# Last pass of a two-layer convolution kernel: its transfers on one queue, its norm chain in seven stages, and a tile's reads dealt over a convolution step

## Chip, cores, metric

The kernel runs on one core of a Trainium2 chip. The metric is device time in microseconds (us). The engines are TensorE (PE for its matmuls, PEld for its weight loads), VectorE (DVE), ScalarE (ACT), GpSimd (POOL) and SyncE (SP). Each executes its own instructions in order. Transfers (DMA) are issued by an engine's instruction stream, here mostly by SyncE and POOL, and so stand in order with everything else on that engine; they all run on the core's 16 DMA engines.

## What is computed

The input x is 8 x 96 x 96 x 192 in float32. There are two residual layers. The part that matters here is the second:

```python
x = x + L0(_gn(x))                       # layer 0
y = conv7x7_depthwise(_gn(x)) + dw_bias  # layer 1; _gn is a group norm over 32 groups of 6 channels
mu = mean(y, axis=-1); var = mean((y - mu)**2, axis=-1)
y = (y - mu) * rsqrt(var + 1e-6) * ln_gamma + ln_beta
y = gelu(y @ w0 + b0)                    # 192 -> 768
y = y @ w1 + b1                          # 768 -> 192
out = x + y * gamma
```

Layer 0 projects 192 channels to 384, applies a 3x3 depthwise convolution and four exponential scans, normalises over the channels and projects back to 192 channels.

## The kernel before

**Stages.** The first three stages compute layer 0. They end with the residual stage (`load_c`, `block_c`, `finish_c`), which writes the sum to the DRAM tensor X (`X1_d`, one part for each half of the batch) and gathers the group norm's sums. Then comes the depthwise convolution of layer 1 (letter d in the code), then the last stage (letter e): norm over the channels, the expansion with gelu ("first layer"), the contraction ("second layer"), the residual and the output.

**Convolution.** It works on 32 tiles `todo[n]`, 16 blocks of 12 channels (`i`) for each half of the batch (`hf`). For a tile, `load_raw(n, t)` reads three pieces `raw` (t = 0, 1, 2), each in two halves of 384 KB, one issued by SyncE and one by POOL; `load_band(n)` reads the weight matrix `band` (624 KB) by SyncE where the block's index i is even and by POOL where it is odd, into one half of the partitions; `scale_steps(n)` gives 24 scalings `xin<-raw` (eight for each piece; they apply the group norm; DVE L838, or ACT L836 for tile 1 and for tiles from 19 on) and ends with a DVE copy of the band into the other half of the partitions (L842). `conv_d(n, c)` is called for c = 0..5: 24 matmuls (L1167) into two PSUM banks, which ACT empties into `yo` with the bias (L1177). `store_d(n)` writes `yo` to the DRAM tensor Y: three stores by SyncE and three by POOL, of which one each has 810 KB and the others 27 KB.

**Buffers of raw.** Before the change, pieces of tile 0 and pieces 0 and 1 of odd tiles and of tiles from 19 on have two buffers in the pool `early`, which lives from before the residual stage on. Even tiles (2 to 18) and piece 2 of odd tiles have four buffers in the pool `own`, which lies where the residual stage's tiles were and opens when that stage is over.

**Order of the convolution.** All order is written out by hand (`tc.manual_schedule()`). Tiles 0 to 18 (`N1` = 19) run alone, with no work of the last stage beside them ("convolution alone"). In the loop over n, each turn issues `store_d(n - 1)`, `load_band(n + 1)`, `load_raw(n + 2, t)` for the three pieces, `scale_steps(n + 1)`, and then the six steps of `conv_d(n, c)`. As soon as tile 15 is stored, the first half of the batch is complete in Y, and the last stage can begin. So in turn n = 16 `load_y(0)` is issued, all 41 steps at once, behind `store_d(15)` and `load_band(17)` and ahead of `load_raw(18, t)`; in turn 18 the norm chain of e-tile 0 is put ahead of the convolution's steps; after the loop come `load_y(1)`, `store_d(18)`, `load_band(19)` and two pieces of raw 19. The bank of PSUM is taken in a ring of eight.

**Last stage.** It has 72 e-tiles u, two for each of the 36 pieces of Y. `load_y(n)` gives 41 steps: one that makes the tiles `ya` and `yb` (two buffers each) and 40 reads from Y by SyncE (32 of 60 KB, L1226, and 8 of 16 KB, L1232, one after each four). The first 20 reads fill `ya`, the others `yb`. `load_r(n)` reads the residual `r` (1536 KB, SyncE, L1243), and `bias_r(n)` adds the output bias to it on POOL (L1249). `norm_steps_e(u)` gives the chain of the norm, before the change in six stages: `sums` (DVE, L1305), `mean` (DVE), `center` (two subtracts on DVE, L1298, and two squares on ACT, L1318), `squares` (DVE, L1324), `powers` (DVE, and a power on POOL, L1330, that gives `rs`), `scale` (small DVE copies `m<-rs` that wait for POOL, and two multiplies at L1298). `turn_in(u, k)`, k = 0, 1, 2, transposes 32x32 blocks on DVE into `yT` (L1351). `first_layer(u, part, ..)` has the expansion's matmuls (L1366 and L1376) and the gelu on ACT (L1385), in three parts in the first half of the e-tiles and in two in the second half. `second_layer(u, k, ..)`, k = 0..3, has 48 matmuls (L1396), the residual add on DVE (L1407, `xo`) and the output's store by POOL (L1415).

**Mixed stage.** A step of the loop over u has the first layer of u, the second layer of u - 1 in four quarters, the norm chain of u + 2 (its last stage, `scale`, in the next step) and the turns of u + 1. Between them `slot()` is called five times. From u = 2 on a slot takes one entry of the list `slots` until that is empty. Each convolution tile from 19 to 31 has nine entries: three with eight scalings each, which also issue the next raw reads (the entry of piece 0 issues `raw (n, 2)`, those of pieces 1 and 2 issue pieces 0 and 1 of tile n + 1), and six with one `conv_d(n, c)` each on two PSUM banks of its own (`ps_y`), of which the last also issues `store_d(n)` and `load_band(n + 1)`. So tile n + 1 begins one slot after tile n's store. A slot also takes up to seven steps of a pending `load_y`. Those are put in line in even steps u, ahead of the fourth slot, so they fall into the fourth and fifth slot of an even step and the first four of the odd step. `load_r` comes after the first slot of odd steps and `bias_r` after the third. Before the change a slot issues its steps of `load_y` first and its convolution entry second. When `slots` is empty, nothing but the last stage is left.

Of the kernel before, what the change touches and what calls it, by code (L numbers as in the profile page):

```python
# [101 lines left out]
def conv_blocks_kernel(  # L102
# [31 lines left out]
    nc = tc.nc  # L134
# [655 lines left out]
    def load_raw(n, t):  # L790

        hf, i = todo[n]
        own = 0 < n < N1 and (n % 2 == 0 or t == NT - 1)
        raw = d_pools[own].tile(
            [128, NH, NV, GC, WQ], F32, tag="raw", name="raw", bufs=4 if own else 2
        )
        raws[n, t] = raw
        row = NGC * NV * GC * WQ
        run = NV * GC * WQ
        x1 = X1_d[hf]  # L800
        for g, eng in enumerate((nc.sync, nc.gpsimd)):
            src = bass.AP(
                tensor=x1.tensor,
                offset=x1.offset + (2 * t + g) * HG * PH * row + i * run,
                ap=[[row, 64], [ROWS * row, NH], [1, run]],
            )
            eng.dma_start(
                raw[g * 64 : (g + 1) * 64].rearrange("q b a c v -> q b (a c v)"), src
            )

    def load_band(n):
# [5 lines left out]
        (nc.sync, nc.gpsimd)[g].dma_start(  # L817
# [4 lines left out]
    def scale_steps(n):  # L822
# [4 lines left out]
        def scale(t, k, b):  # L827
# [7 lines left out]
            if n == 1 or n >= N1:  # L835
# [89 lines left out]
    with ExitStack() as ph:  # L925
# [143 lines left out]
        with tc.manual_schedule():  # L1069
            weights = load_weights()  # L1070
            for u in range(n_u + 1):
# [7 lines left out]
                if u == n_u - 20:  # L1079
                    load_band(0)  # L1080
                    for t in range(NT - 1):
                        load_raw(0, t)
                    first_d += scale_steps(0)
                    for k, (n, t) in enumerate(((0, 2), (1, 0), (1, 1))):
                        first_d.insert(
                            (k + 1) * 8 + k, lambda n=n, t=t: load_raw(n, t)
                        )
# [97 lines left out]
    def store_d(n):  # L1185
# [5 lines left out]
        for k, eng in enumerate((nc.sync, nc.gpsimd)):  # L1191
# [64 lines left out]
    def norm_steps_e(u):  # L1256
# [57 lines left out]
        def center():  # L1314
            apply(ALU.subtract)
            t_["sq"] = sq = sp.tile([128, NH, WE + HV, CK], F32, tag="sq", name="sq", bufs=1)
# [24 lines left out]
        return [sums, mean, center, squares, powers, scale]  # L1341
# [78 lines left out]
    with tc.manual_schedule():  # L1420
        with tc.tile_pool(name="d_own", bufs=1, side="right", **by_tile) as own:
            d_pools[1] = own
            load_raw(1, NT - 1)
            load_band(1)
            norms = norm_c(1, bank)
            for n in range(N1):
# [4 lines left out]
                if n == NI:  # L1431
                    for step in load_y(0):
                        step()
# [4 lines left out]
                if n == N1 - 1:  # L1438
                    for step in norm_steps_e(0):
                        step()  # L1440
                else:
# [3 lines left out]
                    for step in scale_steps(n + 1):  # L1445
                        step()
                for c in range(GS):
                    conv_d(n, c)
            for step in load_y(1):
                step()  # L1450
# [26 lines left out]
        def slot():  # L1477

            for step in loads[:7]:
                step()  # L1480
            del loads[:7]
            if slots and u >= 2:
                for step in slots.pop(0):
                    step()
# [4 lines left out]
        last = norm_steps_e(1)  # L1489
        while len(last) > 1:  # L1490
            last.pop(0)()
        bias_r(0)
        for u in range(n_u + 1):
# [6 lines left out]
            scale_next, last = last[-1], norm_steps_e(u + 2) if u + 2 < n_u else [lambda: None] * 6  # L1500
            first_layer(u, 0, parts, pool)
            scale_next()
            last.pop(0)()
# [4 lines left out]
            turn_in(u + 1, 0)  # L1508
            last.pop(0)()
            slot()  # L1510
            if early_half:
                first_layer(u, 1, parts, pool)
            turn_in(u + 1, 2)
            second_layer(u - 1, 1, pool)
            last.pop(0)()
            slot()
# [5 lines left out]
            if t == 1 and n + 1 < n_y:  # L1522
                bias_r(n + 1)
            if not early_half:
                first_layer(u, 1, parts, pool)
            second_layer(u - 1, 2, pool)
            last.pop(0)()
# [3 lines left out]
            last.pop(0)()  # L1531
            second_layer(u - 1, 3, pool)
            slot()
# [47 lines left out]
```

## Time and profile before

| | us |
|---|---|
| median of three runs | 5646.87 |
| lowest and highest of them | 5640.79, 5653.08 |
| the profiled execution | 5650.55 |
| its span (first to last instruction) | 5648.7 |
| PE busy | 5332.8 |
| DVE busy | 3620.2 |
| ACT busy | 2583.7 |
| POOL busy | 2372.4 |
| end of the residual stage's matmuls | 2643 |
| first and last matmul of the convolution (L1167) | 2643.8, 4133 |
| first matmul of the first layer (L1366) | 3033.9 |
| first matmul of the second layer (L1396) | 3079.4 |

The page divides the span into 40 equal slices of 141 us and gives for each the busy share of an engine in tenths; PEclk is the clock granted to TensorE, in tenths of full speed. In a listing by time, a line has its start in us from the span's start, its length, the engine, the line of the code, the operation with what it writes and reads, and how many like instructions are merged in it. Where an engine was idle before it, square brackets give for how long and what released it. `SPq` is SyncE issuing a transfer: its length is the issue, not the transfer. A group's row gives busy time, the mean length in ns, and the idle time of the engine before its instructions with what ended it.

### The profile page before, as it was taken

The page shows a single profiled execution, that of the slowest core. Times are in us where ns is not written, and L with a number is a line of the kernel's source. Part 1 is how long each engine was busy: PE and PEld are TensorE (multiplying, and loading weights), DVE is VectorE, ACT ScalarE, POOL GpSimd, SP SyncE. Part 2 cuts the span into 40 slices and gives each one's busy share as a digit, 9 for nine tenths or more (in the row PEclk, how much of TensorE's full clock was granted, in tenths as well). Part 3 has the DMA queues.
Part 4 walks back from the last instruction along what each step waited for, and adds up shares of the span by engine and source line. Part 5 has one row for each costly group of instructions (what it writes and reads, how often), then busy time and mean ns, then how long its engine had stood idle before and what let it go on. Part 6 is the DMA issues. An engine that isn't in the chain of part 4 may idle for free. (4 is left out here: it accounts for less than half of the span.)

```text
span 5648.7 us, 108168 instructions
## 1 busy us (share of the span) xinstructions
PE 5332.8 (94%) x42206; PEld 3354.0 (59%) x42206; DVE 3620.2 (64%) x6738; ACT 2583.7 (46%) x5762; POOL 2372.4 (42%) x2122
## 2 busy tenths in 40 slices
PE   6999989999998999998776998989999999999999
PEld 3666633333333999997343555555566677666667
DVE  5556449999998455555455554555567677767764
ACT  2444447777776566565332444434433333333332
POOL 1111128888887555554222332322333333333332
PEclk9999979999999999999887999999999999999999
DMA  7999869999997899999995445455433332233331
GB/s 208 281 287 270 239 176 244 246 244 244 244 246 207 261 295 288 281 289 264 270 269 132 118 118 113 119 121 135 111 82 85 87 86 77 78 85 91 82 78 40
DMA packets 793200, 1015.29 MB, mean 180 GB/s; under 512 B 331840, under 2 KB 674417, under 8 KB 790641
## 3 DMA queue, kind: packets, MB, share of 16 engines
q1 hardware_dynamic: 696664, 640.98, 43.9%
q0 software_dynamic: 90064, 365.17, 20.6%
q8 instruction: 333, 5.46, 0.4%
q10 hardware_dynamic: 5960, 2.22, 0.2%
q14 instruction: 179, 1.46, 0.1%
HBM read 603.70 MB, written 419.95 MB: 181 GB/s over the span
## 5 line engine op out<-in xcount | busy, mean ns | idle before, releaser
L1396 PEld LDWEIGHTS hp<-w1g,g 128*128 128x128 f32 x6912 | 1117.9, 190 | 140.7 <-issue 71.8
L1396 PE MATMUL hp<-w1g,g 128*128 128x192 f32 x6912 | 1174.9, 329 | 0.0
L1385 ACT ACTIVATE g<-hp,b0g 128x512 f32<-128x512 f32 x864 | 518.2, 690 | 771.0 <-PE hp L1376 771.0
L1366 PE MATMUL hp<-yT,w0w 128*128 128x512 f32 x1728 | 788.4, 602 | 22.9 <-DVE yT L1351 13.4
L1415 POOL DMA_DIRECT2D out_dram<-xo x288 | 211.6, 735 | 1393.2 <-DVE xo L1407 1360.2
L1007 PE MATMUL po<-wc,mt 128*128 128x193 f32 x3456 | 683.6, 333 | 2.1 <-DVE x1c L1024 1.8
L1407 DVE TENSOR_TENSOR xo<-hp,r 128x384 f32<-128x384 f32 x288 | 227.8, 791 | 689.7 <-PE hp L1396 688.3
L600 PE MATMUL pl<-pin,band 34*32 34x380 f32 (+1 forms) x13824 | 636.4, 494 | 18.8 <-DMA pin<-P_d 18.8
L1167 PE MATMUL hp<-xin,band 63*64 63x372 f32 (+1 forms) x4608 | 453.9, 529 | 176.5 <-DMA band<-Z_d 63.2
L674 POOL TENSOR_TENSOR mo<-mo,z 128x768 f32<-128x768 f32 x286 | 598.0, 2091 | 3.7 <-ACT mo L625 1.2
L1007 PEld LDWEIGHTS po<-wc,mt 128*128 128x128 f32 x3456 | 553.4, 191 | 33.0 <-ACT mean L1009 30.6
L1366 PEld LDWEIGHTS hp<-yT,w0w 128*128 128x128 f32 x1728 | 324.2, 192 | 392.4 <-issue 358.8
L633 DVE TENSOR_TENSOR_SCAN z<-decay,loc 128x768 f32<-128x768 f32 x288 | 505.8, 1756 | 71.5 <-ACT loc L609 42.7
L642 DVE TENSOR_TENSOR_SCAN z<-decay,z 128x768 f32<-128x768 f32 x288 | 498.4, 1731 | 0.1
L1330 POOL TENSOR_TENSOR rs<-tot,neg_half 32x32 f32<-32x32 f32 x72 | 392.1, 5445 | 194.2 <-DVE tot L1328 193.8
L600 PEld LDWEIGHTS pl<-pin,band 34*32 34x32 f32 x13824 | 233.2, 108 | 403.7 <-issue 402.2
L1167 PEld LDWEIGHTS hp<-xin,band 63*64 63x64 f32 x4608 | 213.4, 146 | 385.3 <-issue 245.2
L621 PE MATMUL pa<-loc,mix 128*32 128x384 f32 x3456 | 436.7, 498 | 0.0
L624 PE MATMUL pa<-last,down 96*32 96x384 f32 x1152 | 431.6, 498 | 0.9 <-ACT mo L625 0.9
L1376 PE MATMUL hp<-yT,w0w 64*128 64x512 f32 x1728 | 419.5, 611 | 0.0
L382 PE MATMUL pm<-xT,win 128*128 128x384 f32 x1152 | 394.1, 492 | 7.8 <-DVE po L406 7.8
L1318 ACT ACTIVATE sq<-ya 128x1024 f32<-128x1024 f32 x72 | 146.3, 2031 | 545.0 <-DVE ya L1298 304.6
(158 smaller groups left out, 7488.1 us busy)
## 6 DMA issues: line engine op xcount, KB each, us to landing
P_d<-po POOLq DMA_DIRECT2D x96, 1152.0 KB, 9.6
pin<-P_d SPq DMA_DIRECT2D x192, 576.0 KB
mt<-M SPq DMA_DIRECT2D x192, 384.0 KB
xq<-in_x_dram SPq DMA_DIRECT2D x96, 576.0 KB
xr<-in_x_dram SPq DMA_DIRECT2D x192, 288.0 KB
X<-x1c SPq DMA_DIRECT2D x144, 384.0 KB
r<-X SPq DMA_DIRECT2D x36, 1536.0 KB
out_dram<-xo POOLq DMA_DIRECT2D x288, 192.0 KB, 2.5
```

Source lines behind the costliest of these rows:

```text
L600: nc.tensor.matmul(pls[g][at * RB : (at + 1) * RB, :, lo:hi], band[rows, c, kh, :], pin[rows, c, :, NJ - 1 - j, lo + kh - 1 : hi + kh - 1] ...
L621: nc.tensor.matmul(pa[at], mix[:, i, at], loc[:, q], start=True, stop=True)
L624: nc.tensor.matmul(pa[at], down[:, to], last[:, q], start=True, stop=True)
L633: nc.vector.tensor_tensor_scan(zf, decay_f, loc.rearrange("p q n -> p (q n)"), 0.0, ALU.mult, ALU.add)
L642: nc.vector.tensor_tensor_scan(zr, decay_f, zr, 0.0, ALU.mult, ALU.add)
L674: eng.tensor_tensor(m, m, z, ALU.add)
L1007: nc.tensor.matmul(po, lhs[m], wc[:, m], start=(m == 0), stop=(m == NC - 1))
L1167: nc.tensor.matmul(pys[g][k * 64 : (k + 1) * 64, :, lo:hi], band[rows, k * GS + c, d * ZS : d * ZS + 64], xin[rows, :, :, k * GS + c, lo + ...
L1366: nc.tensor.matmul(hps[m, q], w0w[:, 0, m * 128 : (m + 1) * 128], yT[:, 2 * q], start=True, stop=False,)
L1376: nc.tensor.matmul(hps[m, q], w0w[p, 1, m * 128 : (m + 1) * 128], yT[p, 1], start=False, stop=True,)
L1385: nc.scalar.activation(g[:, m, q], hps[m, q], AF.Gelu, bias=b0g[:, m : m + 1], scale=1.0)
L1396: nc.tensor.matmul(po[:, q], g[:, m, q, k * 128 : (k + 1) * 128], w1g[:, m], start=(m == 0), stop=(m == NE - 1),)
```

## The change

All of it lies in the convolution of layer 1 and the last stage.

- *Queues.* For tiles from 19 on, both halves of `load_raw`, the band and all six stores of `store_d` are issued by SyncE. Tiles 0 to 18 keep SyncE and POOL.
- *Buffers of raw.* Tile 0 and the odd tiles have pieces 0 and 1 in two buffers of `early` (as tiles from 19 on do) and piece 2 in one buffer of the pool `gp`, which is open in the residual stage already. Even tiles from 2 to 18 have three buffers in `own`. All three pieces of tile 0 are read at once near the end of the residual stage, and all three of tile 1 there too, each as the scaling of tile 0's like piece is past; before, piece 2 of tile 1 was read after that stage.
- *Scaling of tile 18* is done by ACT instead of DVE.
- *Reads of Y.* `load_y(0)` is dealt in portions of seven over the six steps of convolution tile 16, so it stands behind `load_raw(18, t)`. `load_y(1)` is dealt in the same way over tile 18.
- *First norm chains.* The chain of e-tile 0 is put ahead of the steps of convolution tile 17, and that of e-tile 1, all but its last stage, ahead of those of tile 18.
- *Seven stages.* The squares on ACT become a stage of their own, `square`, behind `center`.
- *Order of a step.* A slot issues its convolution entry first and its steps of `load_y` second. `scale` moves from behind the first part of the first layer to behind the second layer's first quarter; the stages of the chain are spread over the step, with `square` behind the third quarter and `powers` at the end; `turn_in(u + 1, 0)` moves behind the first layer's second part, `turn_in(u + 1, 1)` behind the third quarter.

```diff
-        own = 0 < n < N1 and (n % 2 == 0 or t == NT - 1)
-        raw = d_pools[own].tile(
-            [128, NH, NV, GC, WQ], F32, tag="raw", name="raw", bufs=4 if own else 2
-        )
+        if n >= N1 or ((n == 0 or n % 2) and t < NT - 1):
+            pool, bufs = early, NT - 1
+        elif n == 0 or n % 2:
+            pool, bufs = gp, 1
+        else:
+            pool, bufs = d_pools[1], NT
+        raw = pool.tile([128, NH, NV, GC, WQ], F32, tag="raw", name="raw", bufs=bufs)
...
-        for g, eng in enumerate((nc.sync, nc.gpsimd)):
+        for g, eng in enumerate((nc.sync, nc.sync if n >= N1 else nc.gpsimd)):
...
-        (nc.sync, nc.gpsimd)[g].dma_start(
+        (nc.sync, nc.gpsimd)[g and n < N1].dma_start(
...
-            if n == 1 or n >= N1:
+            if n == 1 or n >= N1 - 1:
                 nc.scalar.activation(to, of, AF.Identity, bias=sh, scale=sc)
...
                     load_band(0)
-                    for t in range(NT - 1):
+                    for t in range(NT):
                         load_raw(0, t)
                     first_d += scale_steps(0)
-                    for k, (n, t) in enumerate(((0, 2), (1, 0), (1, 1))):
-                        first_d.insert(
-                            (k + 1) * 8 + k, lambda n=n, t=t: load_raw(n, t)
-                        )
+                    for t in range(NT):
+                        first_d.insert((t + 1) * 9 - 1, lambda t=t: load_raw(1, t))
...
-        for k, eng in enumerate((nc.sync, nc.gpsimd)):
+        for k, eng in enumerate((nc.sync, nc.sync if n >= N1 else nc.gpsimd)):
...
         def center():
             apply(ALU.subtract)
+
+        def square():
             t_["sq"] = sq = sp.tile([128, NH, WE + HV, CK], F32, tag="sq", name="sq", bufs=1)
...
-        return [sums, mean, center, squares, powers, scale]
+        return [sums, mean, center, square, squares, powers, scale]
...
-            load_raw(1, NT - 1)
             load_band(1)
-            norms = norm_c(1, bank)
+            norms, chain = norm_c(1, bank), []
...
-                if n == NI:
-                    for step in load_y(0):
-                        step()
...
-                if n == N1 - 1:
-                    for step in norm_steps_e(0):
-                        step()
-                else:
+                if n + 1 < N1:
                     if n + 2 < N1:
                         for t in range(NT):
                             load_raw(n + 2, t)
                     for step in scale_steps(n + 1):
                         step()
+                if n >= NI + 1:
+                    chain = norm_steps_e(n - NI - 1)
+                    for _ in range(7 if n == NI + 1 else 6):
+                        chain.pop(0)()
+                parts = load_y((n - NI) // 2) if n in (NI, NI + 2) else []
                 for c in range(GS):
                     conv_d(n, c)
-            for step in load_y(1):
-                step()
+                    for step in parts[c * 7 : c * 7 + 7]:
+                        step()
```

The loop over u, after the change (`norm` is the chain of u + 1 with its last stage left, `chain` that of u + 2):

```python
        def slot():
            if slots and u >= 2:
                for step in slots.pop(0):
                    step()
            for step in loads[:7]:
                step()
            del loads[:7]
...
            norm, chain = chain, norm_steps_e(u + 2) if u + 2 < n_u else [lambda: None] * 7
            first_layer(u, 0, parts, pool)
            chain.pop(0)()
            slot()
            if t == 1 and n + 1 < n_y:
                load_r(n + 1)
            second_layer(u - 1, 0, pool)
            norm.pop(0)()
            chain.pop(0)()
            slot()
            if early_half:
                first_layer(u, 1, parts, pool)
            turn_in(u + 1, 0)
            second_layer(u - 1, 1, pool)
            chain.pop(0)()
            slot()
            if t == 1 and n + 1 < n_y:
                bias_r(n + 1)
            if not early_half:
                first_layer(u, 1, parts, pool)
            turn_in(u + 1, 2)
            second_layer(u - 1, 2, pool)
            turn_in(u + 1, 1)
...
            chain.pop(0)()
            slot()
            if early_half:
                first_layer(u, 2, parts, pool)
            chain.pop(0)()
            second_layer(u - 1, 3, pool)
            chain.pop(0)()
            slot()
```

More of the change, by code (lines that the diff above doesn't have):

```diff
@@ L1477, in slot @@
         def slot():
+            if slots and u >= 2:
+                for step in slots.pop(0):
+                    step()
             for step in loads[:7]:
@@ L1481, in slot @@
             del loads[:7]
-            if slots and u >= 2:
-                for step in slots.pop(0):
-                    step()
         load_r(0)
@@ L1488, in conv_blocks_kernel @@
             turn_in(0, k)
-        last = norm_steps_e(1)
-        while len(last) > 1:
-            last.pop(0)()
         bias_r(0)
@@ L1498, in conv_blocks_kernel @@
                 assert not slots
-            scale_next, last = last[-1], norm_steps_e(u + 2) if u + 2 < n_u else [lambda: None] * 6
+            norm, chain = chain, norm_steps_e(u + 2) if u + 2 < n_u else [lambda: None] * 7
             first_layer(u, 0, parts, pool)
-            scale_next()
-            last.pop(0)()
+            chain.pop(0)()
             slot()
@@ L1507, in conv_blocks_kernel @@
             second_layer(u - 1, 0, pool)
-            turn_in(u + 1, 0)
-            last.pop(0)()
+            norm.pop(0)()
+            chain.pop(0)()
             slot()
@@ L1512, in conv_blocks_kernel @@
                 first_layer(u, 1, parts, pool)
+            turn_in(u + 1, 0)
+            second_layer(u - 1, 1, pool)
+            chain.pop(0)()
+            slot()
+            if t == 1 and n + 1 < n_y:
+                bias_r(n + 1)
+            if not early_half:
+                first_layer(u, 1, parts, pool)
             turn_in(u + 1, 2)
-            second_layer(u - 1, 1, pool)
-            last.pop(0)()
-            slot()
+            second_layer(u - 1, 2, pool)
             turn_in(u + 1, 1)
@@ L1521, in conv_blocks_kernel @@
                 loads += load_y(n + 2)
[L1522 to L1527, printed above, removed]
+            chain.pop(0)()
             slot()
@@ L1530, in conv_blocks_kernel @@
                 first_layer(u, 2, parts, pool)
-            last.pop(0)()
+            chain.pop(0)()
             second_layer(u - 1, 3, pool)
+            chain.pop(0)()
             slot()
```

## The prediction

> **What bounds the kernel now.** I read the page's slices first, then busy time by stretch, the groups of TensorE from 3100 to 4135 us, and the order of time around their waits.
>
> ```profile
> PE   6999989999998999998776998989999999999999
> ...
> PEclk9999979999999999999887999999999999999999
> DMA  7999869999997899999995445455433332233331
> ```
>
> One stretch by busy time (length, then busy PE, PEld, DVE, ACT, POOL, clock, DMA share, GB/s):
>
> ```profile
> 4480.00:5580.00 1100.00, 1100.00 (x4972) 764.62 (x4971) 775.50 (x1442) 344.10 (x482) 384.36 (x207) 1.00 0.31 80
> ```
>
> PE is full from 4135 us on, at full clock. No reordering of other engines shortens that. Two stages are left: the convolution alone (2644 to 3025 us, DMA at 9 tenths) and convolution beside the expansion layers (to 4133 us, DMA at half).
>
> The convolution alone starts with a hole. Columns as above:
>
> ```profile
> 2640.00:2660.00 20.00, 14.10 (x121) 8.27 (x119) 14.51 (x40) 10.21 (x27) 3.11 (x3) 0.91 0.62 200
> 2660.00:2680.00 20.00, 5.38 (x45) 3.52 (x49) 1.46 (x1) 8.40 (x18) 3.08 (x5) 0.57 0.87 215
> 2680.00:2700.00 20.00, 11.98 (x152) 7.63 (x144) 7.18 (x24) 7.37 (x14) 6.71 (x11) 0.88 0.91 217
> 2700.00:2720.00 20.00, 14.77 (x144) 6.50 (x144) 9.77 (x26) 6.31 (x12) 5.72 (x7) 0.84 1.01 287
> ```
>
> It ends with another: SyncE works through the 40 reads of `load_y(0)`, and behind them stand the reads of raw and the band of tile 18 (time, length, engine, line):
>
> ```profile
> 2995.56 1.93 SPq L807 DMA_DIRECT2D raw<-X  x3
> ...
> 2999.07 2.55 SPq L817 DMA_DIRECT2D band<-Z_d  x1
> ...
> 3009.16 15.97 PE L1167 MATMUL hp<-xin,band 63*64 63x384 f32 x144 [30.82 <-DMA band<-Z_d]
> ```
>
> In the mixed stage the convolution's matmuls wait 73.8 us in 13 places; 45.1 and the 9.8 (its weight load names xin) are for scaled input, 18.9 for evacuation:
>
> ```profile
> L1167 PE MATMUL hp<-xin,band 63*64 63x384 f32 (+1 forms) x1872 | 191.8, 531 | 73.8 <-ACT xin L836 45.1 <-ACT yo L1177 18.9 <-DVE m L1290 9.8
> ```
>
> The evacuation kind: the bias add on POOL holds the subtract on DVE (6.53 us instead of 1.22), the square on ACT waits for it, and the evacuation stands behind the square:
>
> ```profile
> 3175.34 5.44 POOL L1249 TENSOR_TENSOR r<-r,b1g 128x3072 f32<-128x3072 f32 x1
> 3175.35 6.53 DVE L1298 TENSOR_TENSOR yb<-yb,m 128x1024 f32<-128x1024 f32 x1
> ...
> 3181.91 1.11 ACT L1318 ACTIVATE sq<-yb 128x512 f32<-128x512 f32 x1 [4.36 <-DVE yb L1298]
> ...
> 3183.41 4.00 PE L1167 MATMUL hp<-xin,band 63*64 63x384 f32 x24 [3.79 <-ACT yo L1177]
> ```
>
> The input kind: POOL issues its half of a tile's third read early, SyncE is still busy with a Y store and reads of yb:
>
> ```profile
> 3265.86 2.16 SPq L1198 DMA_DIRECT2D Y<-yo  x1
> ...
> 3270.33 7.65 SPq L1226 DMA_DIRECT2D yb<-Y  x4
> ...
> 3273.83 0.66 POOL L807 DMA_DIRECT2D raw<-X  x1
> ...
> 3286.09 8.99 SPq L807 DMA_DIRECT2D raw<-X  x3
> ...
> 3290.87 3.61 ACT L836 ACTIVATE xin<-raw,s 128x192 f32<-128x192 f32 x8 [9.00 <-DMA raw<-X]
> ...
> 3294.10 4.46 PE L1167 MATMUL hp<-xin,band 63*64 63x384 f32 x24 [9.78 <-DVE m L1290]
> ```
>
> [...] beside the power (L1330) the add out of PSUM keeps its 0.79 us. [...] 24 convolution matmuls take 2.13 us, after a wait 4.0 to 4.46. [...]
>
> **Part by part**, against the profiled execution: 5650.55 us, its span 5648.7 plus 1.85 around it. The median shown, 5646.87, is 3.7 lower.
>
> 1. Reads of raw (1, 2) move from after the residual stage into it. In 2660 to 2700 us DMA moved 20 x (215 + 217) = 8640 KB; at some 275 GB/s, the saturated stretches' rate, that takes 31.4 us: 8.6 gained. It can be gained because today tile 1's scaling waits 15.97 us on ACT for raw (1, 2) and the evacuation of tile 0, the Y store behind it, and the band and raw after that store all start late. The 786 KB leave this stage: 2.9 more. They cost 2.7 at 290 GB/s where they go, as DMA is full there too. **-9 us**; ends 0 (the hole only moves) and -13.
>
> 2. End of the convolution alone. raw (18) now precedes `load_y(0)`, but band (18) still follows it on SyncE (i = 2 is even), so it lands about 3003 instead of 3009: 6 gained. The norm chain of tile 0 stands on DVE behind that band's copy, so it starts only as much earlier, and its square now stands on ACT ahead of tile 17's evacuation, tile 1's ahead of tile 18's. With eight banks four of six convolution steps pass, then PE waits. From row durations: chain of tile 0 3004.5 to 3027 (22.2 as today), tile 1's square done 3037, last convolution steps 3042, turns done 3043: first layer at 3043, today 3033.9. `load_y(1)` waits for the store of tile 17, so it starts 3023 instead of 3006 and lands about 3063; the sums of tile 2 hold DVE until then, and 13 us of DVE work (2.9 sums, 3.4 scale, 2.5 mean, 2.4 center, three turns of 1.05) lead to the next first layer. Second layer at some 3082, today 3079.4. What is late next is that read. **+3 us**; ends -6 and +9. Scaling tile 18 on ACT instead of DVE costs 24 x 0.54 = 13 us under ACT's wait for that chain, so nothing.
>
> 3. Square as a stage of its own. It goes behind the next evacuation, before slot four, while the bias add still meets the subtract. The five waits of 3.8 us go, and with each the slow restart (4.0 against 2.13): 5 x 5.7 = **-28 us**. Ends -34 (with tile 19's wait, where the square alone stood ahead of scaling) and -15. Its cover is 4.2 us of second layer; powers now end the step and the 5.45 us power runs under the next one, where DVE waits 5 us for it today. Turn 1 moves behind the second layer's third quarter: in the PE-full stage four us of second layer and some four of first layer remain over it, DVE is 70% busy there: nothing, at worst 2.
>
> 4. Transfers of the mixed stage on SyncE. POOL loses 141 + 45 us of waits; of its work only the bias add ends a PE wait, so that alone brings nothing. Per tile SyncE gets three more stores (0.32 + 0.35 + 2.16), three raw reads (0.58 each), every second band (2.2): 5.7 us of issue, while today it waits 456 of 1035 us for other engines (the sum of its waits on ACT and DVE in this stage). [...] POOL's half took 13.3 us to land, so I take 14 from the evacuation T. And of slot work and its batch of seven reads of Y, the slot work now goes first: between a store and the next raw still lies one batch, the one before. Four cases. Tile 21 (and 31): measured, scaling ended at T + 30.5 (3264 to 3294.5); 2.5 us of bytes and four more reads at 0.47 make it 4 later. Tile 20 (and 30): today no batch is between; then the last one is, with yb: bytes gone at T + 14, batch landed T + 22, raw 7 later, scaling 3.6: T + 33, while three expansion parts (5.6 each) and three quarters (4.2) need it at T + 29.4: 3.5 late. Tile 23: the batch between has no wait for landing any more, 5 gained; tile 26: none between, 5 gained. Tiles 19 and 29: the square no longer stands ahead of scaling, 4 and 2 gained. Tile 24 loses 1.5, 22 and 25 three together. Waits: 54 + 8 + 7 - 10 - 6 + 4.5 = 58, and nine restarts of 2.3 instead of seven: 71 become 79. **+8 us**; ends -60 and +60[...].
>
> 5. New order of buffers (three own instead of four, one early): each is free before its next read; nothing.
>
> Sum: -9 + 3 - 28 + 8 = -26, so 5624.5 for this execution and 5621 beside the median.
>
> **Rivals.** *Raw in time*: putting raw ahead of each batch is worth more than the bytes ahead of it cost, as POOL's halves of raw landed in 6.8 us in the median, 4.6 at best. Then 50 of the 71 us go: -9 + 3 - 28 - 50 = -84, 5563. Against it: batches still precede. *One queue backs up*: each raw stands behind store, band and batch; ten of twelve tiles wait 10 us and restart, 123 instead of 71: -9 + 3 - 28 + 52 = +18, 5665, slower. It decides once those waits exceed 71 + 34 + 11 = 116 us. Against it: SyncE's idle time. *Gains given back*: the start's hole only moves (0), the end costs 9, evacuation gains 15, queue costs 8: +2, 5649, no change.
>
> **Numbers.** Forecast 52%, own range 5600 to 5640; raw in time 22%; backs up 13%; given back 13%. A measurement of this kernel can tell about 0.2%, 11 us. Faster: 46 + 22 = 68%; slower: 13 and 2 of the third case = 15%; the rest 17%. Range: half of the fast case and most of the slow one in, 5560 to 5664.
>
> **What would show it.** Step 1: DMA near 1.0 from 2660 us, no 16 us wait of ACT for raw. Step 2: `band` of 18 right behind `load_y(0)`, evacuation of 17 behind a square. Step 3: no evacuation waits of 3.8 us at the matmuls, subtracts of 6.5 us still there. Step 4: waits for xin near 58 us, moved to tiles 20 and 30. I am wrong if the PE-full stage lengthens, if xin waits vanish or double, or if a wait for r or Y takes their place.

## The result, and the profile after

The changed kernel takes 5588.73 us in the median (5586.89 to 5589.95, 4 runs), the kernel before 5647.91 beside it (5640.79 to 5653.08, 4 runs): a ratio of 0.9896, 95% interval 0.9879 to 0.9913, so 59 us or 1.0% faster (49 to 68 us). The forecast was 26 us. The direction and most signs of the steps hold, the size does not. The profiled execution took 5586.89 us with a span of 5585.1, against 5650.55 and 5648.7.

A table of stages shows where the difference lies. I cut both traces at matmuls that the change leaves alone: the last `pm` of the first stage, the last `pa` of the second, the last of the residual stage (`po<-wc`), the first convolution matmul of tile 17, the first second-layer matmul (`hp<-w1g,g`), the last convolution matmul, the end.

| stretch | before, us | after, us | difference |
|---|---|---|---|
| first stage | 763.7 | 756.2 | -7.5 |
| second stage | 1053.6 | 1041.2 | -12.5 |
| residual stage | 826.4 | 829.8 | +3.4 |
| convolution alone, to tile 17 | 321.3 | 314.3 | -7.0 |
| tile 17 to second layer | 114.3 | 117.6 | +3.3 |
| mixed stage, to the last convolution | 1054.5 | 1011.4 | -43.1 |
| PE-full stage | 1514.8 | 1514.6 | -0.2 |

Two things stand out. The mixed stage gained twice the 20 us that steps 3 and 4 allowed it. And 20 us came from two stages whose code is the same in both kernels. The rest fell near the forecast; PE-full is unchanged to 0.2 us.

The slices of the changed kernel (the 40th parts of a shorter span, so they don't line up exactly):

```profile
PE   6999989999998999998775999999999999999999
...
PEclk9999989999999999999887999999999999999999
DMA  7999869999997899999995554565433332233331
```

By stretches (length, then busy PE, PEld, DVE, ACT, POOL, granted clock, DMA share, GB/s):

```profile
2640.00:2660.00 20.00, 7.48 (x74) 4.07 (x70) 5.22 (x14) 4.35 (x10) 6.91 (x10) 0.69 0.88 226
2660.00:2680.00 20.00, 18.00 (x213) 10.66 (x209) 10.62 (x33) 9.08 (x18) 4.92 (x7) 0.97 1.04 314
2680.00:2700.00 20.00, 14.79 (x152) 7.02 (x148) 11.48 (x35) 6.58 (x13) 4.40 (x6) 0.83 1.04 321
```

From 2660 us DMA is full at 314 GB/s, where it moved 215 before: the hole at the start of the convolution alone is closed, as step 1 said. (From tile 0 to tile 2 this is 12 us, as the next table shows; over the whole stretch to tile 17 the profiles differ by only 7.0, but that stretch also takes 307 to 314 us in traces whose code is the same up to there.)

At its end, the queue of SyncE and, from other views, PE and DVE:

```profile
2917.68 10.78 SPq L810 DMA_DIRECT2D raw<-X  x3
2932.05 10.70 SPq L1227 DMA_DIRECT2D ya<-Y  x4
...
2973.39 1.72 SPq L820 DMA_DIRECT2D band<-Z_d  x1
```

```profile
2991.69 13.89 PE L1168 MATMUL hp<-xin,band 63*64 63x384 f32 x144 [40.76 <-ACT yo L1178]
3013.62 7.29 PE L1168 MATMUL hp<-xin,band 63*64 63x384 f32 x48 [8.04 <-ACT yo L1178]
...
3048.54 2.05 PE L1369 MATMUL hp<-yT,w0w 128*128 128x512 f32 x2 [10.99 <-DVE yT L1354]
```

```profile
3040.58 1.01 DVE L1306 TENSOR_REDUCE s<-yb 128x16 f32<-128x512 f32 x1 [19.31 <-DMA yb<-Y]
```

raw (18) leads, the 40 reads of `load_y(0)` and the band follow, and the convolution now waits for evacuations that stand behind the squares of tiles 0 and 1. The 10.99 us before the next first layer come from the read of `load_y(1)` that step 2 named as late next: DVE waits 19.31 us for it in the sums of tile 2.

The convolution's matmuls in the mixed stage (busy, mean ns, then idle time before them and what ended it):

```profile
L1168 PE MATMUL hp<-xin,band 63*64 63x372 f32 x1248 | 121.6, 494 | 0.0
L1168 PE MATMUL hp<-xin,band 63*64 63x384 f32 x624 | 75.9, 531 | 41.4 <-ACT xin L839 20.9 <-DVE band L845 20.4
```

41.4 us where 73.8 stood: no wait for an evacuation is left, and the waits for input, forecast at 58, are 41.4. The collision itself is still there, as forecast, but nothing hangs on it any more:

```profile
3153.01 5.45 POOL L1250 TENSOR_TENSOR r<-r,b1g 128x3072 f32<-128x3072 f32 x1
3153.01 6.54 DVE L1299 TENSOR_TENSOR yb<-yb,m 128x1024 f32<-128x1024 f32 x1
...
3153.23 1.05 ACT L1178 ACTIVATE yo<-hp,dwb 128x384 f32<-128x384 f32 x2 [4.61 <-PE hp L1168]
...
3157.21 2.13 PE L1168 MATMUL hp<-xin,band 63*64 63x384 f32 x24
...
3159.58 1.12 ACT L1321 ACTIVATE sq<-yb 128x512 f32<-128x512 f32 x1 [3.39 <-DVE yb L1299]
```

The subtract takes 6.54 us beside the bias add, but the evacuation (L1178) goes ahead of the square, and the next convolution step starts on time and takes 2.13 us.

The prediction named a wait for Y as a sign of being wrong. There is one, on DVE: its sums wait 88.7 us in the mixed stage for reads of Y, and 2.4 before. On PE little of it is seen: apart from the convolution's, its one wait of any length in this stage is 3.9 us at 3090 us.

### The profile page after: what moved, and what is told of

The parts are those of the page before. It is cut to its first block, busy times and chain, and to the rows that moved or that the text cites. A ratio compares the mean times of both kernels' runs of the same rounds, so it can differ in the third digit from the quotient of the medians.

```text
span 5585.1 us, 108130 instructions
## 1 busy us (share of the span) xinstructions
PE 5299.5 (95%) x42206; PEld 3348.2 (60%) x42206; DVE 3594.6 (64%) x6714; ACT 2594.4 (46%) x5786; POOL 2326.4 (42%) x2037
## 5 line engine op out<-in xcount | busy, mean ns | idle before, releaser
L1168 PE MATMUL hp<-xin,band 63*64 63x372 f32 (+1 forms) x4608 | 441.8, 521 | 154.7 <-DVE band L845 53.4
L1178 ACT ACTIVATE yo<-hp,dwb 128x384 f32<-128x384 f32 x384 | 200.3, 576 | 437.3 <-PE hp L1168 359.1
L609 ACT COPY loc<-pl 128x384 f32<-128x384 f32 x576 | 248.1, 483 | 311.6 <-PE pl L600 311.6
```

The source lines that it names most:

```text
L1168: nc.tensor.matmul(pys[g][k * 64 : (k + 1) * 64, :, lo:hi], band[rows, k * GS + c, d * ZS : d * ZS + 64], xin[rows, :, :, k * GS + c, lo + ...
```

## The experiments

Twelve kernels, in three groups of four. Most vary one part of the changed kernel, or add one part to the kernel before; e7 and e9 vary several. Medians of the kernel before on these occasions: 5652.98 (e1 to e4), 5648.78 (e5 to e8), 5649.79 (e9 to e12).

Most steps are not much larger than the scatter of whole executions (the kernel before ran from 5633 to 5669 us beside e1 to e4), so each trace, one execution for each kernel, was cut as above as well. "Start" is tile 0 to tile 2 of the convolution, "end" tile 17 to the first second-layer matmul, "mixed" from there to the last convolution matmul.

| kernel | first stage | second stage | residual, own matmuls | start | end | mixed | median us, ratio (95%) |
|---|---|---|---|---|---|---|---|
| before | 763.7 | 1053.6 | 806.1 | 56.8 | 114.3 | 1054.5 | see above |
| after | 756.2 | 1041.2 | 809.9 | 44.7 | 117.6 | 1011.4 | 5588.7, 0.9896 (0.9879 to 0.9913) |
| e1 | 754.7 | 1043.6 | 807.8 | 45.4 | 118.2 | 1068.8 | 5639.8, 0.9980 (0.9972 to 0.9988) |
| e2 | 754.4 | 1047.4 | 810.0 | 45.3 | 123.9 | 1003.0 | 5584.3, 0.9884 (0.9868 to 0.9900) |
| e3 | 755.0 | 1041.2 | 808.2 | 45.5 | 119.1 | 1007.5 | 5574.6, 0.9870 (0.9852 to 0.9888) |
| e4 | 753.6 | 1046.6 | 808.8 | 44.9 | 117.6 | 1016.8 | 5589.0, 0.9889 (0.9873 to 0.9905) |
| e5 | 764.4 | 1059.9 | 803.0 | 57.4 | 114.1 | 1003.8 | 5601.8, 0.9911 (0.9895 to 0.9927) |
| e6 | 764.4 | 1040.1 | 803.9 | 58.3 | 117.1 | 1056.6 | 5651.3, 1.0001 (0.9990 to 1.0013) |
| e7 | 753.8 | 1040.7 | 810.7 | 45.1 | 121.2 | 1000.6 | 5576.1, 0.9864 (0.9846 to 0.9882) |
| e8 | 753.3 | 1053.8 | 809.9 | 44.4 | 108.3 | 1014.8 | 5576.1, 0.9870 (0.9851 to 0.9889) |
| e9 | 751.9 | 1050.0 | 806.8 | 45.2 | 116.3 | 1000.4 | 5565.7, 0.9851 (0.9836 to 0.9866) |
| e10 | 765.9 | 1054.2 | 803.1 | 58.5 | 114.2 | 1024.1 | 5614.2, 0.9934 (0.9919 to 0.9949) |
| e11 | 755.0 | 1040.7 | 801.2 | 57.0 | 115.9 | 1055.2 | 5628.6, 0.9960 (0.9946 to 0.9975) |
| e12 | 754.7 | 1041.4 | 810.9 | 45.5 | 116.2 | 1053.2 | 5619.8, 0.9950 (0.9935 to 0.9965) |

**e1: the square back behind the subtract**, in the changed kernel.

```
 def center():
     apply(ALU.subtract)
+    square_1()
+
 def square():
+    pass
+
+def square_1():
     t_["sq"] = sq = sp.tile([128, NH, WE + HV, CK], F32, tag="sq", name="sq", bufs=1)
     ...
```

> The changed kernel, with the square back on ACT right behind the subtract (the stage of its own left empty). Theory of the prediction: the square's place is what removes the five waits of 3.8 us for evacuation and their slow restarts, 5 x 5.7 = 28 us, so this kernel takes 5589 + 28 = 5617 us (5604 to 5623) and its matmuls wait some 19 us for yo again. Rival, the mixed stage's gain of 43 us comes from the transfers and the order of the step alone: within 5 us of 5589, no waits for yo. If the 20 us gained ahead of the residual stage are a property of the changed program, the end of the second stage stays near 1797 us here; if they are scatter between executions, it can come anywhere from 1797 to 1818.

Measured 5639.8 us: 51 more than the changed kernel, not 28. The mixed stage is 57 us longer, and its convolution waits 77.2 us, 15.6 of them for yo. The rival is out. The square's place is the change; all the rest together leaves 11 us (0.9980, so 7 to 16 below the kernel before), and 9 of them are in the first stage.

**e5: the square's stage alone**, in the kernel before. A step pops one stage more, behind the second layer's last quarter; turns and slots stay.

```
 def center():
     apply(ALU.subtract)
+
+def square():
     ...
-return [sums, mean, center, squares, powers, scale]
+return [sums, mean, center, square, squares, powers, scale]
```

> The kernel before, with one thing done: the square is a stage of its own behind the second layer's third quarter, squares and powers one place later; queues, order of a slot, turns, reads of raw and the end of the convolution alone as before. New theory, from the run with the square put back: the square's place is worth 51 us in the mixed stage (evacuation waits with restarts 24, input waits of the tiles whose scaling stood behind a waiting square some 20, their restarts the rest): some 5602 us, the mixed stage's input waits under 45 us. Prediction: 28, so 5625. If the 20 us of the first two stages belong to the program (this one has the first stages of the kernel before), the second stage ends near 1817 us; if they are scatter, it ends near 1798 in this trace or the next.

5601.8 us, the ratio 0.9911 being 50 us (41 to 59); its mixed stage is 50.7 us shorter than before. e1 and e5 agree from both sides: step 3 is worth some 51, not 28. e1 moves the square alone, so it isn't the later place of `squares` and `powers` in e5 that counts. The convolution's matmuls before, and in e5:

```profile
L1167 PE MATMUL hp<-xin,band 63*64 63x372 f32 x1248 | 131.6, 520 | 0.0
L1167 PE MATMUL hp<-xin,band 63*64 63x384 f32 x624 | 81.6, 555 | 73.8 <-ACT xin L836 45.1 <-ACT yo L1177 18.9 <-DVE m L1290 9.8
```

```profile
L1167 PE MATMUL hp<-xin,band 63*64 63x372 f32 x1248 | 120.7, 487 | 0.0
L1167 PE MATMUL hp<-xin,band 63*64 63x384 f32 x624 | 76.8, 526 | 39.8 <-ACT xin L836 35.4 <-DVE band L842 3.3 <-ACT g L1387 1.0
```

Waits -34.0, busy -15.7 (6 slow convolution steps, of over 3 us, instead of 12), together -49.7. Of the waits 18.9 are the evacuations; 16 are waits for input at seven tiles, which the forecast had not given to this step (1.0 comes back as a wait for the gelu). One of them, tile 26, shows how. The kernel before, at the last convolution step of tile 25:

```profile
3653.67 2.12 PE L1167 MATMUL hp<-xin,band 63*64 63x384 f32 x24
...
3655.80 2.06 ACT L1318 ACTIVATE sq<-ya 128x1024 f32<-128x1024 f32 x1 [4.56 <-issue]
...
3657.62 1.12 ACT L1318 ACTIVATE sq<-yb 128x512 f32<-128x512 f32 x1
3658.53 1.03 ACT L1177 ACTIVATE yo<-hp,dwb 128x384 f32<-128x384 f32 x2
...
3659.59 0.32 SPq L1193 DMA_DIRECT2D Y<-yo  x1
...
3674.27 0.58 SPq L807 DMA_DIRECT2D raw<-X  x1
...
3683.30 3.61 ACT L836 ACTIVATE xin<-raw,s 128x192 f32<-128x192 f32 x8 [6.95 <-DMA raw<-X]
```

and e5 at the same place:

```profile
3641.14 2.12 PE L1167 MATMUL hp<-xin,band 63*64 63x384 f32 x24
...
3643.32 1.05 ACT L1177 ACTIVATE yo<-hp,dwb 128x384 f32<-128x384 f32 x2 [4.61 <-PE hp L1167]
...
3644.40 0.32 SPq L1193 DMA_DIRECT2D Y<-yo  x1
...
3657.99 0.58 SPq L807 DMA_DIRECT2D raw<-X  x1
...
3665.59 3.61 ACT L836 ACTIVATE xin<-raw,s 128x192 f32<-128x192 f32 x8 [1.78 <-DMA raw<-X]
```

No bias add is near. Counted from the convolution step on PE, the evacuation starts 4.9 us later in the kernel before and 2.2 in e5, the store of Y 5.9 and 3.3, the read of raw behind it 20.6 and 16.9, and the scaling of the last piece 29.6 and 24.5. The square stands in ACT's order ahead of the tile's last evacuation; behind that stand store, band and raw. The evacuation is 2.7 us earlier in e5, the last scaling 5.2; of these PE gets 3.0 (its wait at tile 26 falls from 7.7 to 4.7). Why the lead grows behind the store is not shown.

**e10: the bias add one quarter later**, in the kernel before; the square stays.

```
-            if t == 1 and n + 1 < n_y:
-                bias_r(n + 1)
...
             second_layer(u - 1, 2, pool)
             last.pop(0)()
+            if t == 1 and n + 1 < n_y:
+                bias_r(n + 1)
```

> The kernel before, with the bias add on POOL issued one quarter of the second layer later, so that it no longer meets the subtract; the square stays right behind the subtract. Prediction's account (the bias add holds the subtract, the square and with it the evacuation): the five evacuation waits of 3.8 us and their restarts go, 28 us, so 5625 us; waits for input stay near 55 us. If the whole 51 us of the square's place come from that collision: 5602. If it is the square's place in ACT's queue alone, with or without the bias add: within 8 us of 5650 and the evacuation waits stay.

The mixed stage is 30.4 us shorter, the total 37 (29 to 46). The row:

```profile
L1167 PE MATMUL hp<-xin,band 63*64 63x372 f32 x1248 | 122.7, 500 | 0.0
L1167 PE MATMUL hp<-xin,band 63*64 63x384 f32 x624 | 76.9, 540 | 56.0 <-ACT xin L836 56.0
```

All five evacuation waits are gone, and the waits for input stay, 56.0 against 54.9. So the collision cost what the forecast said, 28 us there and 30 here. The other 20 of the 51 come with the square's place and not with the bias add, since moving the bias add leaves them; that it is the place in ACT's order is read from tile 26.

**e2, e3, e6, e7: queue and order of a slot.** e2 is the changed kernel with two queues for raw, band and Y, e3 with the reads of Y ahead of the slot's own work, e7 with both; e6 is the kernel before with one queue.

e2 and e7 (e6 has the same edits the other way round, in the kernel before):

```
-for g, eng in enumerate((nc.sync, nc.sync if n >= N1 else nc.gpsimd)):
+for g, eng in enumerate((nc.sync, nc.gpsimd)):
...
-(nc.sync, nc.gpsimd)[g and n < N1].dma_start(
+(nc.sync, nc.gpsimd)[g].dma_start(
...
-for k, eng in enumerate((nc.sync, nc.sync if n >= N1 else nc.gpsimd)):
+for k, eng in enumerate((nc.sync, nc.gpsimd)):
```

e3 and e7:

```
-if slots and u >= 2:
-    for step in slots.pop(0):
-        step()
 for step in loads[:7]:
     step()
 del loads[:7]
+if slots and u >= 2:
+    for step in slots.pop(0):
+        step()
```

> The changed kernel, with the mixed stage's transfers of raw, band and Y dealt over SyncE and POOL as before. The prediction put the single queue, with the order of a slot, at +8 us: undone, 5581 us. New theory, a tile's two halves in one queue land together and ahead of the batch, which gives the 15 to 20 us by which the mixed stage beat its forecast: undone, 5604 to 5609 us, waits for input back from 41 to some 55 us. If only the order of a slot matters, not the queue: within 5 us of 5589.

> The changed kernel, with the seven reads of Y of a slot ahead of the slot's own work as before, all on SyncE still. If the order of a slot carries the 15 to 20 us: 5604 to 5609 us and tiles 23 and 26 wait for input some 8 us more each. If the single queue carries them: within 5 us of 5589. By the prediction's cases of step 4, tiles 23 and 26 lose 5 each and tiles 20 and 30 gain 3.5 each: 5592.

> The kernel before, with one thing done: the mixed stage's raw, band and stores of Y all from SyncE. The prediction gave the queue and the slot order +8 us together; the changed kernel with two queues was 4 us quicker than with one. So 5653 + 4 = 5657 us. Rival, the queue alone brings some of the gain beside the old place of the square: 5640 or less. End of the second stage as in the run above: 1817 if it belongs to the program.

> The changed kernel, with two queues and the reads of Y of a slot ahead of its own work, both as before. If the two losses add: 5589 - 4 - 14 = 5571 us. If they are the same loss[...]: near 5575, the time of the reads first alone. If the old order needs the single queue: above 5580.

After the result I had turned step 4 round, and expected the queue to carry the surprise. That theory falls: e2 comes to 5584.3 and not 5604 or more, and e3's 5574.6 lies below all three of its expectations. Undone, the queue makes the mixed stage 8.4 us shorter, the order 3.9, both 10.8. But part of this only changes place. The first layer's wait for `load_y(1)`, ahead of the mixed stage, is 10.99 us in the changed kernel and 17.00 with two queues (e2; 17.47 in e7), and the changed kernel waits 3.89 right behind it, which the traces with two queues don't:

```profile
3055.36 2.05 PE L1369 MATMUL hp<-yT,w0w 128*128 128x512 f32 x2 [17.00 <-DVE yT L1354]
```

```profile
3089.98 3.70 PE L1369 MATMUL hp<-yT,w0w 128*128 128x512 f32 x8 [3.89 <-DVE xo L1410]
```

With the stretch "end", which is longer by 6.3, 1.5 and 3.6 us, the three traces gain 2.1, 2.4 and 7.2 us. By whole medians it is 4, 14 and 13, with intervals that overlap, so how the loss divides is not told apart. That there is one is: every execution of e3 and e7 (5567 to 5582 us) is below every one of the changed kernel (5587 to 5590). In the kernel before, the queue alone makes no difference that these runs can tell (1.0001, 0.9990 to 1.0013, so 7 us either way; 4 were forecast). Tile by tile, waits in us in the first step of a tile's convolution (the main ones):

| tile | before | e5: square alone | after | e7: no queue, no order |
|---|---|---|---|---|
| 19 | 4.1 | 1.2 | 0.9 | 0.9 |
| 20 | 0 | 0 | 2.6 | 0 |
| 21 | 9.8 | 8.4 | 9.9 | 8.5 |
| 23 | 15.1 | 13.6 | 6.3 | 14.1 |
| 24 | 4.6 | 2.7 | 4.9 | 3.7 |
| 26 | 7.7 | 4.7 | 1.3 | 2.4 |
| 29 | 4.1 | 1.0 | 1.7 | 0.9 |
| 30 | 0 | 0 | 2.3 | 0 |
| 31 | 9.0 | 6.8 | 9.7 | 6.1 |

Between e5 and after the cases of step 4 can be seen: tiles 20 and 30 lose (2.6 and 2.3; 3.5 forecast), 21 and 31 too (1.5 and 2.9; 4 forecast), 23 gains 7.3 (5 forecast), 26 gains 3.4 (5 forecast). It is the picture of the forecast, on a base that lies 16 us lower. Tile 21 in the changed kernel, where the batch now stands between band and raw:

```profile
3248.50 1.38 SPq L820 DMA_DIRECT2D band<-Z_d  x1
3249.93 1.42 SPq L1227 DMA_DIRECT2D yb<-Y  x2
...
3258.09 1.25 SPq L810 DMA_DIRECT2D raw<-X  x2
...
3265.22 3.61 ACT L839 ACTIVATE xin<-raw,s 128x192 f32<-128x192 f32 x8 [6.55 <-DMA raw<-X]
...
3271.01 4.04 PE L1168 MATMUL hp<-xin,band 63*64 63x384 f32 x24 [9.89 <-DVE band L845]
```

**e4 and e12: the reads of raw.** e4 is the changed kernel with tile 1's reads issued after the residual stage; e12 is the kernel before with step 1 alone, buffers and places.

The edit of e4 (e12's is the change's own hunks on the buffers and reads of raw):

```
-                    for t in range(NT):
-                        first_d.insert((t + 1) * 9 - 1, lambda t=t: load_raw(1, t))
...
             d_pools[1] = own
+            for t in range(NT):
+                load_raw(1, t)
             load_band(1)
```

> The changed kernel, with the three reads of raw of tile 1 issued together at the start of the convolution alone and none of them in the residual stage. Prediction, step 1: the start of the convolution alone is worth 12 us gross and costs 2.7 to 3.8 in the residual stage, so 5589 + 9 = 5598 us, the residual stage near 806 us instead of 810. As all three pieces come late here, where the kernel before had only the third late, it can be more: up to three reads of 786 KB at some 275 GB/s, 8.6 us, so 5607. Rival, the hole only moves: within 3 us of 5589.

> The kernel before, with step 1 alone: the buffers of raw as changed (three own, one beside the constants) and tile 1's three reads dealt over the last steps of the residual stage. Prediction: -9 us. By the stage lengths so far: start of the convolution alone -12, residual stage +5, first stage -10 by the moved constants: -17, so 5633 us. Rival, the hole only moves: first stage -10 alone, 5640.

e4 costs nothing: 5589.0 us, start 44.9. Its reads stand after the residual stage in the code, but POOL issues them at 2579.8, 2591.9 and 2600.7 us, inside that stage, as in the changed kernel (2576.7, 2589.1, 2601.5): with the buffers free, POOL ran ahead of the stage. The kernel before issues raw (1, 2) at 2663.8, 20 us after the end of that stage; its buffer lay in the pool that opens when the residual stage has closed. So the buffers are the change, and the place of the reads is not. e12 against e11 gives step 1 by itself: start 11.5 us shorter, median 8.8 lower, though the two ratios' intervals overlap (0.9935 to 0.9965, 0.9946 to 0.9975). Over all traces the residual stage's matmuls take 809 us with the early reads and 804 without, so net it is -6 to -9.

**e8: the old end of the convolution alone**, in the changed kernel.

Reads and scaling in the `else` branch stay as they are; all of chain 1 but its last stage follows the first turns.

```
+if n == NI:
+    for step in load_y(0):
+        step()
...
-if n + 1 < N1:
+if n == N1 - 1:
+    for step in norm_steps_e(0):
+        step()
+else:
...
-if n >= NI + 1:
-    chain = norm_steps_e(n - NI - 1)
-    for _ in range(7 if n == NI + 1 else 6):
-        chain.pop(0)()
-parts = load_y((n - NI) // 2) if n in (NI, NI + 2) else []
 for c in range(GS):
     conv_d(n, c)
-    for step in parts[c * 7 : c * 7 + 7]:
-        step()
...
+for step in load_y(1):
+    step()
```

> The changed kernel, with the end of the convolution alone as before: all reads of the first Y tile ahead of the reads of raw and the band of tile 18, norm chain 0 ahead of tile 18's convolution, the reads of the second Y tile after it, chain 1 after the first turns. Prediction, step 2: the new end costs 3 us, so 5586 us. Ends by the same working: 5580 to 5595. The first layer starts some 9 us later and the second layer 3 us earlier than in the changed kernel, counted from the start of tile 17.

```profile
2992.08 17.31 PE L1168 MATMUL hp<-xin,band 63*64 63x384 f32 x192 [32.24 <-ACT yo L1178]
3015.54 5.67 PE L1369 MATMUL hp<-yT,w0w 128*128 128x512 f32 x8 [6.15 <-DVE yT L1354]
```

With the old end the convolution runs through without the second wait for an evacuation, and from tile 17 to the second layer it takes 108.3 us, 9.3 less than the changed kernel; 3.4 are given back in the mixed stage. So the new end costs 6 to 9 us here, twice the forecast or more and within its bounds; with two queues and the reads first it costs 5 (e9 against e7). Between the two profiles only +3.3 showed, because the other parts of the change shorten this stretch (e8 is 6.0 below the kernel before). Queue and order are these: e9, with the old end and both undone, takes 116.3. The expectation has one sign the wrong way round: the new end was to make the first layer later. In e8 it begins 65.3 us after tile 17, in the changed kernel 79.3.

**e11: one unused buffer**, in the kernel before.

```
 gp = gn_pool.enter_context(tc.tile_pool(name="gn", bufs=1, side="right", **by_tile))
+pad = gp.tile([128, NH, NV, GC, WQ], F32, name="pad_raw")
 blk = gp.tile([128, 128], F32, name="blk")
```

> The kernel before, with one unused buffer of raw's size allocated ahead of the constants blk and pick, in their pool; nothing is read into it. Theory for the first stage: the larger pool puts those constants elsewhere in SBUF, DVE's memset of blk no longer stands in the first stage waiting 9.6 us for the store of Z_d, and the first stage ends near 754 us instead of 764; so 5650 - 10 = 5640 us, the rest as before. Rival, it is something else of the changed program (its queues, its transfers): the first stage still ends near 764.

This one is about the first stage. There the kernel before has a wait of DVE that belongs to another stage:

```profile
91.99 0.17 DVE L939 MEMSET blk<- 128x128 f32 x1 [9.59 <-DMA Z_d<-z]
```

`blk` is a constant of the residual stage. Its memset stands in DVE's order among the first stage's instructions. It ran when the store `Z_d<-z` had landed, after 9.59 us, and what stood behind it waited as well: DVE's next instruction starts at 92.07 us. That `blk` was to take over the memory of that store is inferred from e11: with the padding the wait is gone, and the same memset comes at the end of the first stage:

```profile
754.35 1.14 DVE L406 TENSOR_SCALAR po<-pm,bin__126 128x384 f32<-128x384 f32 x2 [3.50 <-PE pm L395]
755.47 0.17 DVE L940 MEMSET blk<- 128x128 f32 x1
```

The first stage ends at 755.0 us instead of 763.7. In all fourteen traces it ends at 763.7 to 765.9 with the old size of that pool (four) and at 751.9 to 756.2 with a raw buffer more in it (ten). The changed kernel puts such a buffer there (`gp`), so some 10 us of its gain are a by-product of where its buffers lie. The total falls by 23 us (14 to 31), which is more than the first stage alone. The second stage may hold the rest: at its start the granted clock was 0.50 for a time that differs from one trace to the next (until 790 us in the changed kernel and in e11, 820 in the kernel before, 840 in e5), and its first 600 matmuls take 57 to 77 us in these traces. With the old layout they took 71, 77, 57 and 71, with the new 58 to 71, 62 in the mean. So the end of the second stage, on which e5 and e6 were to decide, is 1824 us in one and 1805 in the other, with the same layout. The mean granted clock of whole executions points to a part of the layout in this, 0.972 to 0.974 in e11's six and 0.967 to 0.972 in the eleven of the kernel before beside them, but it doesn't say in which stage. Four and ten traces don't settle it.

**e9: the losses undone**, the changed kernel with e2's, e3's and e8's edits together.

> The changed kernel with the three parts undone that cost time by the runs so far: two queues, the reads of Y of a slot ahead of its own work, and the end of the convolution alone, all as before; the buffers and reads of raw, the square's stage and the turns as changed. If the losses add, 5589 - 13 for queue and order - 9 for the end = 5567 us. If the end's loss comes back elsewhere: 5576 us, as with two queues and reads first alone.

5565.7 us, the forecast of the sum: 1.5% below the kernel before (0.9836 to 0.9866) and 23 us below the changed kernel by the medians. It beats both. That it meets the sum so closely is in part luck: in its trace the edited stretches are 1.3 (end) and 11.0 us (mixed) shorter than in the changed kernel, 12 of the 22 expected. That it beats e7 isn't clear of noise, as the two intervals overlap.

## Why the prediction was wrong, and where it was right

| step | forecast | measured | from |
|---|---|---|---|
| 1, early raw | -9 | -6 to -9 | e12 against e11, stages of all traces |
| 2, end of the convolution alone | +3 | +5 to +9 | e8 to after, e9 to e7 |
| 3, square | -28 | -51 | e1, e5 |
| 4, queue and order | +8 | +8 to +11 in the mixed stage, +7 with the end | e5 to after, e7 to after |
| 5, buffers | 0 | -10 in the first stage, -23 (-14 to -31) in all | e11 |

From these ranges sums between -47 (-6 + 9 - 51 + 11 - 10) and -79 (-9 + 5 - 51 + 7 - 31) can be made; the measured -59, -49 to -68, lies among them. So the table agrees with the result, but the result doesn't fix the smaller terms. The new places of `scale` and of the turns were varied by no run alone; the mixed stage of e7 and e9, which have them, is 3 us shorter than e5's.

**Step 3 is the step that failed**, in its size. "The five waits of 3.8 us go, and with each the slow restart" was right to 2 us (e10). The slow restart was a convolution step at a lower granted clock: in the kernel before, the step at 3173.39 us took 2.12 us at 1.00, the one at 3183.41, after 3.79 us of waiting, 4.00 at 0.58, and the one at 3294.10, after 9.78, 4.46 at 0.50. What failed is the list: it held only waits of PE that the profile labelled `yo`. ACT's own waits at the square, which the working never summed, come to 134.2 us in the mixed stage, in 30 waits, and 18 of them have no bias add near. They fall to 49.9 in e5. The rows before and in e5 (what waited, for what, total, times, longest):

```profile
ACT sq L1318 <- DVE ya L1298: 62.8, 14, 5.0
...
ACT sq L1318 <- issue: 45.2, 10, 4.6
ACT sq L1318 <- DVE yb L1298: 26.2, 6, 4.4
```

```profile
ACT sq L1320 <- DVE yb L1298: 30.8, 8, 5.1
...
ACT sq L1320 <- DVE ya L1298: 12.2, 4, 5.4
ACT sq L1320 <- issue: 6.9, 3, 4.8
```

Such waits delayed what stood behind them on ACT: scaling at tiles 19 and 29, which I did count, under step 4, at 6 us (2.9 + 3.1 measured in e5); and the last evacuation of a tile, which I did not. With those 6 the forecast for what e5 does was 34, and 17 are missing: 10 of them are waits for input at tiles 21, 23, 24, 26 and 31, and 6 are busy time (15.7 less, where five restarts, 9.4, were counted). Step 4 measured everything from "the evacuation T" and took T as given, while step 3 was moving it. The two steps were worked as a sum, but one shifts the other's origin.

**Step 5 failed too.** "Each is free before its next read; nothing" looked at the moved buffers and not at their neighbours. One more buffer in the pool of `blk` is worth 10 us in the first stage (e11). A view that points to it was there: a wait of `blk`, line 939, in a stage that ends at 764 us although its line lies in the residual stage's code.

**Step 1** was right in size, and its cause was half seen: the early place of the reads is nothing by itself, the buffers are all (e4). **Step 2** named the right next wait, the read of `load_y(1)`, and the evacuations behind the squares; alone it costs 5 to 9, and that the profiles show +3.3, as forecast, is luck (9.3 from the end, -6.0 from the other parts). **Step 4** was right in sign and, by tiles, in its cases; after the result I doubted it wrongly. Its 8 included the 6 gained at tiles 19 and 29, which came with the square, so for queue and order alone the forecast was some 14, more than the 8 to 11 measured.

**The rivals.** "Raw in time" needed the waits for input to go with the queue; they went in part, with the square. "One queue backs up" needed over 116 us of such waits with their restarts; there are 41 of waits, some 55 with six restarts of 2.3. "Gains given back" put the evacuations at 15 us; without the collision alone 30 came back (e10). Two readings bore weight and held. The subtract took 6.53 us beside the bias add in the kernel before (at 3175.35 us) and 1.22 at the same place in e10, which parts them (3174.50). And one queue in place of two brought neither gain nor loss beyond 7 us (e6). That bytes queued ahead of a read of raw delay it was my estimate under step 4; no run isolates it.

## What to carry to other kernels

When an instruction is moved in an engine's order, sum the waits of that engine at that instruction, not only the waits of the bounding engine that carry its name. Here these were 134 us and 19, and 51 came back: what was queued behind the square moved too, and at tile 26 the last scaling, at the end of that queue, moved by more (5.2 us) than the evacuation right behind the square (2.7). Steps that are costed from a common event must say whether another step moves that event. When buffers change place, look for waits of unrelated lines whose memory moves along, and compare stages that the change does not touch.

## What the runs showed of the hardware that was not expected

- In the kernel before, a 0.17 us memset held DVE for 9.6 us, until a store had landed, and cost some 10 us of a stage that does not use its result. With one unused buffer more in its pool (e11) the wait was gone.
- At the start of the second stage the clock was 0.50 from 770 to 820 us in the kernel before with PE busy all of 790 to 820; the changed kernel is back at 1.00 from 800 us. The same 600 matmuls took 57 to 77 us over fourteen traces.
- Moving POOL's half of raw, band and Y to SyncE's queue made no difference that can be told in the kernel before: 1.0001 (0.9990 to 1.0013). In the changed kernel it moved a wait: the first layer that needs `load_y(1)` waited 17.00 us with two queues (e2) and 10.99 with one.
